# Four chained image layers on one core: first samples' group norms computed a layer earlier, filter stores on GpSimd's queue, a buffer of its own for the single tap's hats, channel sums taken by ScalarE

## The chip, the core and the metric

The kernel runs on one core of one Trainium2 chip. The core has five engines with instruction queues of their own: TensorE (PE; its weight loads are shown apart as PEld), VectorE (DVE), ScalarE (ACT), GpSimd (POOL) and SyncE (SP). PE multiplies matrices into PSUM, the three element-wise engines work on the on-chip memory SBUF, and SP here only issues DMAs, which 16 DMA engines carry out. ACT and POOL can issue DMAs too. Every queue is worked in order: an instruction that waits holds up all behind it.

The metric is the device time of one execution in microseconds. All arithmetic is float32.

## The reference

The input x has 8 samples of 384 channels and 32x32 positions. Four layers follow one another, each of the form x = x + f(group_norm(x)), where the group norm has 32 groups of 12 channels:

```python
x = x + mamba(_gn(x), ...)                 # layer 0
x = x + deform(_gn(x), ...)                # layer 1
x = x + layernorm_mamba_mlp(_gn(x), ...)   # layer 2
x = x + shift_filter(_gn(x), offset)       # layer 3

def _gn(v, G=32, eps=1e-5):
    g = v.reshape(B_, G, C_ // G, H_, W_)
    m = jnp.mean(g, axis=(2, 3, 4), keepdims=True)
    s = jnp.var(g, axis=(2, 3, 4), keepdims=True)
    return ((g - m) / jnp.sqrt(s + eps)).reshape(v.shape)
```

Layers 0 and 2 are state-space layers: a projection to 768 inner channels, a causal convolution of three taps, a scan h = dA * h + dB * u along the 1024 positions for 16 states per channel, a gate and a projection back; layer 2 also has a layer norm in front and an MLP behind. Layer 1 cuts the channels in three blocks of 128 and gives each a deformable depthwise convolution of size K = 3, 5 and 7. Offsets come from an ordinary KxK convolution of the block, every tap then samples the image bilinearly at its shifted place, and a 1x1 convolution follows. A squeeze-and-excitation weight scales the result: it needs each channel's mean and maximum over the positions. Layer 3 shifts groups of channels by given offsets and filters them.

## The kernel before

Channels lie on the 128 partitions in three groups (`G = 3`), positions along the free dimension. Between layers x is kept in DRAM, one tensor per layer.

**Group norm.** `gn_bn` takes DVE's statistics over halves of 512 positions, `gn_aggr` joins them, `gn_mean` (L151) averages mean and variance over a group of channels with a constant matrix `gmat` on PE, `gn_dev` (L171, L173) gives the deviations on DVE, `gn_square` (L178) squares them on ACT, `gn_mean2` (L161) averages the squares on PE, `gn_sum` (L183) and `gn_rstd` (L192 to L195, ACT) give a factor and an offset for each channel. `gn_mean` and `gn_mean2` multiply all nine pairs of 128-channel groups.

**State-space layers** (`ssm_layer`, L211). The work is 16 half-samples ("steps") of 48 units. A unit is a scan of two states on DVE (L546), with its decays on ACT (L526), its inputs on POOL (L534) and the product with C on DVE (L559) or POOL (L557); PE sums the states (L569). `plan` writes by hand, for each step, what each engine does beside unit t: the output projection of the step before, the gate of this one, and the norm, projection and convolution of the next one. Where the next step begins a sample, its x is loaded at t = 0 and its norm runs from t = 2 to t = 9 (`norm_stats`, L303). The last step has no next one. The first step's norm stands alone ahead of the units, at the start of the layer.

**Deformable layer** (`deform_fast`, L1060). Sample 0 is loaded first (L1066). `fir_weights` then loads the 7x7 offset weights (ACT's queue), forms differences of them on POOL (L1201, L1203) and stores the 121 resulting filters in DRAM in nine pieces on ACT's queue (L1209). They serve a fast form of the 7x7 convolution, here called FIR. The loads of the constants of K = 3 and 5 stand on SP's queue, those of K = 7 on ACT's. This part and all of SP's and POOL's instructions are put in order by the framework's scheduler; ACT, PE and DVE keep the order that is written after it.

That order is by slots. A sample has 46 units: 6 for K = 3, 14 for K = 5, 26 for K = 7. `block_steps` puts work into slots with three places before a slot's unit (`act0`, `pe0`, `dve0`) and three after it (`act1`, `dve1`, `pe1`). With t0 the first unit of a sample and s0 that of a block:

- the sample's load at t0-29, statistics to t0-26, means, squares and factors to t0-21 (`stats` L1238, `rstd`), the norm itself (`norm`, L1262) next;
- the 3x3 convolution for offsets at t0-17, the 5x5 one from t0-14 (`conv`, L1382), the FIR in 16 pieces from t0-5, each loaded three slots earlier (`fir_load` L1310, `fir` L1320, `fir_take` L1330 to L1355, `fir_end`);
- around a block change: transposes of the image (L1417, L1424), then, at s0, `sums_act` (L1461) and `sums` (L1466), which empty the accumulators `wacc` of the block before, the 1x1 convolution (L1472, L1478), `squeeze` (L1485 to L1487), and at the end of a sample the scale (L1527) and the store.

A unit samples one quarter (or, for a set with a single tap, one half) of a set of up to eight taps. ACT computes "hats" max(0, 1 - |p - i|) along x and y from the positions (`hats_x` L1665, L1670; `hats_y` L1682, L1687), DVE multiplies them (L1722, into the ring `fsm` of 7 tiles) and weighs the image (L1705), and PE multiplies and adds into `wacc` (L1759). A block begins with its single-tap set, which has two units. Its x hats and those of the other sets share the ring `fhx` of two tiles. For a set whose first unit is u the positions are loaded at u-5 (L1650), x hats come at u-3 and u, y hats at u-2 and u-1.

If an offset is too large for the fast form, `deform_layer` runs instead; it isn't run on this input.

Of the kernel before, what the change touches and what calls it, by code (L numbers as in the profile page):

```python
# [8 lines left out]
F32 = mybir.dt.float32  # L9
AF = mybir.ActivationFunctionType  # L10
ALU = mybir.AluOpType
# [4 lines left out]
P = 128  # L16
# [86 lines left out]
class Net:  # L103
# [12 lines left out]

    def col(self, i):
        return self.cols[:, i : i + 1]
# [28 lines left out]
    def gn_mean(self, mv):  # L147
        ps = self.psum("gn_ps", n=3 * G)
        for g in range(G):
            for k in range(G):  # L150
                self.nc.tensor.matmul(  # L151
                    ps[:, 2 * g : 2 * g + 2], self.gmat[:, k, g * P : (g + 1) * P], mv[:, k, :],
                    start=(k == 0), stop=(k == G - 1),
                )
        return ps

    def gn_mean2(self, dm):
        ps = self.psum("gn_ps2", n=G)
        for g in range(G):
            for k in range(G):  # L160
                self.nc.tensor.matmul(  # L161
                    ps[:, g : g + 1], self.gmat[:, k, g * P : (g + 1) * P], dm[:, k : k + 1],
                    start=(k == 0), stop=(k == G - 1),
# [47 lines left out]
    def ssm_layer(self, li, src, dst, shift=None):  # L211
# [5 lines left out]
        with ExitStack() as ctx:  # L217
# [74 lines left out]
            def norm_load(s):  # L292
                s["xl"] = []
                for h in (1, 0) if s["h"] == 0 else (1,):
                    x = p2.tile([P, G, TS], F32, name="x", tag="x")
                    nc.sync.dma_start(out=x, in_=src(s["b"])[:, :, h * TS : (h + 1) * TS])
# [391 lines left out]
            def plan(prev, s, nxt):  # L688
# [30 lines left out]
                put(pe, 0, norm_load, nxt)  # L719
                if nxt and nxt["h"] == 0:  # L720
                    put(dve, 2, norm_stats, nxt, 0)
                    put(dve, 3, norm_stats, nxt, 1)
                    put(dve, 3, lambda n: n.update(gn_mv=self.gn_aggr(n["gn_st"])), nxt)
                    put(pe, 4, lambda n: n.update(gn_ps=self.gn_mean(n["gn_mv"])), nxt)
                    put(dve, 5, lambda n: n.update(gn_grp=self.gn_dev(n["gn_mv"], n["gn_ps"])), nxt)
                    put(act, 6, lambda n: n.update(gn_dm=self.gn_square(n["gn_grp"][1])), nxt)
                    put(pe, 6, lambda n: n.update(gn_ps=self.gn_mean2(n["gn_dm"])), nxt)
                    put(dve, 8, lambda n: n.update(gn_var=self.gn_sum(n["gn_grp"][0], n["gn_ps"])), nxt)
                    put(act, 9, lambda n: n.update(gn=self.gn_rstd(n["gn_grp"][0], n["gn_var"])), nxt)
# [55 lines left out]
            with tc.manual_schedule(engines=ENGINES):  # L785
# [3 lines left out]
                for i in range(2):  # L789
                    norm_stats(s, i)  # L790
                s["gn"] = s["sib"]["gn"] = self.gn_finish(s["gn_st"])
# [130 lines left out]
    def deform_layer(self, src, dst):  # L922
        tc, nc, ins = self.tc, self.nc, self.ins
        with ExitStack() as ctx:
# [26 lines left out]
            for b in range(self.nb):  # L951
# [28 lines left out]
                for g in range(G):  # L980
                    nc.vector.scalar_tensor_tensor(
                        x[:, g, :], og[:, g, :], se[:, g : g + 1], x[:, g, :], ALU.mult, ALU.add
                    )
                nc.scalar.dma_start(out=dst(b), in_=x)
# [75 lines left out]
    def deform_fast(self, src, dst):  # L1060
        tc, nc, ins = self.tc, self.nc, self.ins
        with ExitStack() as ctx:
# [67 lines left out]
            for u, (b, g, j, h) in enumerate(units):  # L1130
                if h == 0:
                    one = self.parts(g, j) == 2
                    loads[u - 5] = b, g, j
                    for t, fn, k in (
                        ((-3, self.hats_x, 0), (-2, self.hats_y, 0), (-1, self.hats_y, 1))
                        if one
                        else ((-3, self.hats_x, 0), (-2, self.hats_y, 0), (-1, self.hats_y, 1), (0, self.hats_x, 1))
# [966 lines left out]
```

## Time and profile before

| what | value |
|---|---|
| median of 3 runs | 8860.76 us (8858.26 to 8862.39) |
| the profiled execution's own time | 8859.41 us |
| its span, first to last instruction | 8857.3 us |
| mean granted clock of TensorE | 0.906 |
| busy: PE, DVE, ACT, POOL | 84%, 85%, 66%, 63% of the span |

The page of a profile gives busy times by engine and the costliest groups of instructions; the trace behind it answers questions. In a timeline, a row has the start and the duration in microseconds, the engine, the line of the kernel, the operation, what it writes and reads, and how many instructions are merged; brackets hold the idle time of the engine before it, and what ended that time as far as semaphores tell. ACTq and SPq are DMA instructions on the queues of ACT and SP, where the duration of a merged row runs from its first to its last issue. In a row of groups, the busy time and the mean nanoseconds of one instruction follow the count. Durations come from one execution.

### The profile page before, as it was taken

The page shows a single profiled execution, that of the slowest core. Times are in us where ns is not written, and L with a number is a line of the kernel's source. Part 1 is how long each engine was busy: PE and PEld are TensorE (multiplying, and loading weights), DVE is VectorE, ACT ScalarE, POOL GpSimd, SP SyncE. Part 2 cuts the span into 40 slices and gives each one's busy share as a digit, 9 for nine tenths or more (in the row PEclk, how much of TensorE's full clock was granted, in tenths as well). Part 3 has the DMA queues.
Part 4 walks back from the last instruction along what each step waited for, and adds up shares of the span by engine and source line. Part 5 has one row for each costly group of instructions (what it writes and reads, how often), then busy time and mean ns, then how long its engine had stood idle before and what let it go on. Part 6 is the DMA issues. An engine that isn't in the chain of part 4 may idle for free. (4 is left out here: it accounts for less than half of the span.)

```text
span 8857.3 us, 91757 instructions
## 1 busy us (share of the span) xinstructions
PE 7449.8 (84%) x29880; PEld 3853.8 (44%) x29880; DVE 7519.8 (85%) x8477; ACT 5818.6 (66%) x9453; POOL 5565.4 (63%) x3374
## 2 busy tenths in 40 slices
PE   7888888888884899999999975788888888888886
PEld 2232233233221788788788861233333333333332
DVE  6999999999995788988898886888898988888872
ACT  6777777777773656665665655676777777676740
POOL 6999999999996000000000006998898989999954
PEclk8899899899897999999999997898898989999988
DMA  4554555445544554464446434566666566566646
GB/s 127 123 125 120 129 122 124 121 119 124 126 121 112 145 135 125 112 163 131 112 129 159 123 87 104 130 153 150 159 154 149 146 145 154 143 156 157 158 135 112
DMA packets 805681, 1177.71 MB, mean 133 GB/s; under 512 B 267010, under 2 KB 423842, under 8 KB 771400
## 3 DMA queue, kind: packets, MB, share of 16 engines
q1 hardware_dynamic: 742980, 1155.63, 53.0%
q10 hardware_dynamic: 62212, 16.13, 0.9%
q8 instruction: 238, 3.90, 0.2%
q14 instruction: 251, 2.06, 0.1%
HBM read 982.54 MB, written 188.98 MB: 132 GB/s over the span
## 5 line engine op out<-in xcount | busy, mean ns | idle before, releaser
L534 POOL TENSOR_TENSOR db<-dub,bc 128x1024 f32<-128x1024 f32 x1536 | 3608.1, 2358 | 370.7 <-DVE hs L546 170.3
L526 ACT ACTIVATE da<-dtb,vec 128x512 f32<-128x512 f32 x3072 | 2123.4, 691 | 603.1 <-DVE hs L559 403.7
L546 DVE TENSOR_TENSOR_SCAN da<-da,db 128x1024 f32<-128x1024 f32 x960 | 2193.3, 2285 | 130.5 <-ACT da L526 84.0
L467 POOL TENSOR_TENSOR dt<-dt,sp_e 128x512 f32<-128x512 f32 x96 | 122.4, 1275 | 2546.7 <-DVE sp_e L459 2546.7
L1759 PE MATMUL wacc<-fsm,fxk 128*128 128x195 f32 (+21 forms) x10624 | 1575.1, 306 | 151.0 <-ACT fhy L1682 77.2
L1759 PEld LDWEIGHTS wacc<-fsm,fxk 128*128 128x128 f32 x10624 | 1475.9, 195 | 286.9 <-DVE fsm L1722 152.6
L546 DVE TENSOR_TENSOR_SCAN hs<-da,db 128x1024 f32<-128x1024 f32 x576 | 1315.3, 2284 | 195.4 <-POOL db L519 80.8
L557 POOL TENSOR_TENSOR hs<-hs,bc 128x1024 f32<-128x1024 f32 x576 | 1357.8, 2357 | 33.4 <-ACT st L552 33.4
L559 DVE TENSOR_TENSOR hs<-da,bc 128x1024 f32<-128x1024 f32 x960 | 1175.6, 1225 | 126.8 <-PE y L569 77.0
L569 PE MATMUL y<-hs,cols 128*32 128x512 f32 x6144 | 984.0, 650 | 280.3 <-POOL hs L557 258.4
L1722 DVE TENSOR_TENSOR fsm<-fhy,fhx 128x143 f32<-128x143 f32 (+40 forms) x3280 | 1081.9, 397 | 66.8 <-PE wacc L1759 53.0
L1705 DVE TENSOR_TENSOR fxk<-fxt,fwk 128x1024 f32<-128x1024 f32 (+1 forms) x688 | 814.3, 1184 | 10.4 <-PE wacc L1759 5.6
L1682 ACT ACTIVATE fhy<-fpyx,cell 128x416 f32<-128x416 f32 (+10 forms) x832 | 423.8, 582 | 373.7 <-DVE fsm L1722 373.4
L569 PEld LDWEIGHTS y<-hs,cols 128*32 128x32 f32 x6144 | 190.1, 113 | 1006.8 <-issue 491.9
L646 PE MATMUL ps_m<-hid,wm 128*128 128x512 f32 x1152 | 549.3, 632 | 61.9 <-ACT hid L641 27.8
L627 PE MATMUL ps_h<-t,wm 128*128 128x512 f32 x1152 | 530.9, 605 | 44.1 <-DVE sp_e L459 24.6
L1665 ACT ACTIVATE fhx<-fpyx,cell 128x416 f32<-128x416 f32 (+10 forms) x664 | 372.2, 630 | 257.2 <-DVE fsm L1722 252.8
L359 PE MATMUL ps_in<-xn,winr 128*128 128x512 f32 x576 | 327.1, 714 | 174.3 <-ACT xn L348 125.7
L646 PEld LDWEIGHTS ps_m<-hid,wm 128*128 128x128 f32 x1152 | 226.3, 202 | 394.2 <-issue 280.0
L627 PEld LDWEIGHTS ps_h<-t,wm 128*128 128x128 f32 x1152 | 216.1, 193 | 363.0 <-issue 271.5
L578 PE MATMUL ps_z<-xn,winr 128*128 128x512 f32 x576 | 303.0, 674 | 47.8 <-DVE sp_e L459 47.8
L1687 ACT ACTIVATE fhy<-fhy,cols 128x1184 f32<-128x1184 f32 (+8 forms) x208 | 307.6, 1479 | 6.8
(227 smaller groups left out, 9815.7 us busy)
## 6 DMA issues: line engine op xcount, KB each, us to landing
dtb<-dtd SPq DMA_DIRECT2D x768, 256.0 KB
dub<-dtd SPq DMA_DIRECT2D x768, 256.0 KB
fpyx<-fposd SPq DMA_DIRECT2D x104, 1024.0 KB
fxt<-fxd SPq DMA_DIRECT2D x96, 1024.0 KB
wm<-in_w SPq DMA_DIRECT2D x96, 768.0 KB
bc<-bcd SPq DMA_DIRECT2D x256, 256.0 KB
x<-x SPq DMA_DIRECT2D x71, 768.0 KB
dtd<-dt SPq DMA_DIRECT2D x192, 256.0 KB
```

The source lines that it names most:

```text
L526: nc.scalar.activation(da[:, i, :], s["dtb", j][:, k, :], AF.Exp, scale=na[:, j, n + i : n + i + 1])
L534: nc.gpsimd.tensor_tensor(db, du, s["bc"][p][:, 0], ALU.mult)
L546: nc.vector.tensor_tensor_scan(h1, da1, db1, 0.0, ALU.mult, ALU.add)
L557: nc.gpsimd.tensor_tensor(s["hs", m], s["hs", m], c, ALU.mult)
L559: nc.vector.tensor_tensor(hs_tile(s, m), s["da", m], c, ALU.mult)
L569: nc.tensor.matmul(s["y"][k * IP : (k + 1) * IP, :], sel, s["hs", p * NSUB + k][:, i, :], start=mlp and p == 0 and i == 0, stop=p == NQP - ...
L627: nc.tensor.matmul(ps, s["w1", q][:, k, f * P : (f + 1) * P], s["t"][:, k, :], start=(k == 0), stop=(k == G - 1))
L646: nc.tensor.matmul(ps, s["w2", q][:, f, o * P : (o + 1) * P], s["hid", q][:, f, :], start=(f == 0), stop=(f == 3))
L1682: nc.scalar.activation(hy[:, at : at + (yb - ya) * W], s["pyx", j][:, 0, ya * W : yb * W], AF.Abs, bias=bias)
L1705: nc.vector.tensor_tensor(t[:, :n], x, wk[:, j : j + 1, :].to_broadcast([P, n, P]), ALU.mult)
L1722: nc.vector.tensor_tensor(self.sub(sm, at, [(r * w, n), (w, r), (1, w)]), self.sub(hy, hy_at[by] + xa, [(r * W, n), (W, r), (1, w)]), self ...
L1759: nc.tensor.matmul(a[:, ya - 4 * o : yb - 4 * o, xa:xb], k, self.sub(sm, sm_at[by], [(w, yb - ya), (1, w)]), start=o not in s["open"], sto ...
```

## The change

1. Layer 0's last step carries the norm of sample 0 of layer 1, as if it were a next step: two loads of x, the statistics, and so on. The result goes to a new constant tile `gns`. Layer 1 then leaves out this sample's statistics.
2. Sample 0 of layer 1 gets statistics of its output (in `scale`), and its norm for layer 2 is finished 17 to 21 slots after its end, that is in sample 1. Layer 2 then starts with the norm at hand.
3. In `gn_mean` and `gn_mean2` the two pairs of groups that are not neighbours are left out (a group of 12 channels spans at most two of them): 7 products for 9.
4. The nine filter stores go out on GpSimd's queue. For sample 0 the FIR begins two slots later.
5. The single tap's x hats get a buffer `fhs`; the first set after it has its x hats one slot earlier and its positions' load is written one slot earlier; the ring `fsm` has 6 tiles.
6. The channel sums come from the accumulator of ACT's instruction that writes `fog`, in two halves that DVE adds; DVE's sum over 1024 positions is left out.

```diff
+        t = self.const.tile([P, 4, G], F32, name="gns")
+        self.gns = {li: (t[:, li - 1], t[:, li + 1]) for li in (1, 2)}
...
     def gn_mean(self, mv):
-            for k in range(G):
+            ks = [k for k in range(G) if abs(k - g) < 2]
+            for k in ks:
...
# plan, in ssm_layer
-                put(pe, 0, norm_load, nxt)
-                if nxt and nxt["h"] == 0:
-                    put(dve, 2, norm_stats, nxt, 0)
...
+                nn = nxt if nxt or mlp else {"b": 0, "h": 0, "src": dst}
+                put(pe, 0, norm_load, nn)
+                if nn and nn["h"] == 0:
+                    put(dve, 2, norm_stats, nn, 0)
...
+                    to = () if nxt else self.gns[1]
+                    put(act, 9, lambda n: n.update(gn=self.gn_rstd(n["gn_grp"][0], n["gn_var"], *to)), nn)
...
# start of a state-space layer
-                for i in range(2):
-                    norm_stats(s, i)
-                s["gn"] = s["sib"]["gn"] = self.gn_finish(s["gn_st"])
+                if mlp:
+                    s["gn"] = s["sib"]["gn"] = self.gns[2]
+                else:
+                    for i in range(2):
+                        norm_stats(s, i)
+                    s["gn"] = s["sib"]["gn"] = self.gn_finish(s["gn_st"])
...
# deform_fast
-                    loads[u - 5] = b, g, j
+                    lead = 4 if j == 0 else 3
+                    loads[u - 5 if one or j else u - 6] = b, g, j
...
-                        else ((-3, self.hats_x, 0), (-2, self.hats_y, 0), (-1, self.hats_y, 1), (0, self.hats_x, 1))
+                        else ((-lead, self.hats_x, 0), (-2, self.hats_y, 0), (-1, self.hats_y, 1), (0, self.hats_x, 1))
...
# fir_weights
-            nc.scalar.dma_start(out=o, in_=w[:, r0:r1, c0:c1, :].rearrange("p r c o -> p r (c o)"))
+            nc.gpsimd.dma_start(out=o, in_=w[:, r0:r1, c0:c1, :].rearrange("p r c o -> p r (c o)"))
...
# block_steps
-                sample["xn"] = self.xn0
+                sample["xn"], sample["gn"] = self.xn0, self.gns[1]
...
         def point_act():
+            s["sum"] = self.q2.tile([P, 2], F32, name="fos")
-                nc.scalar.activation(og[:, sl], s["pw"][h], AF.Identity, bias=pwb[:, g : g + 1])
+                nc.scalar.activation(
+                    og[:, sl], s["pw"][h], AF.Identity, bias=pwb[:, g : g + 1], accum_out=s["sum"][:, h : h + 1]
+                )
...
-            nc.vector.reduce_sum(am[:, g, 0:1], og, axis=AX.X)
+            nc.vector.tensor_tensor(am[:, g, 0:1], s["sum"][:, 0:1], s["sum"][:, 1:2], ALU.add)
...
         def scale(k):
+            if b == 0:
+                if k == 0:
+                    sample["st"] = self.q1.tile([P, G, 2, 6], F32, name="gn_st0")
+                for h, sl in halves():
+                    nc.vector.bn_stats(sample["st"][:, k, h, :], xr[:, sl])
...
-            put(t0 - 6, "dve1", fir_sum)
-            t = t0 - 5
+            t = t0 - 5 if b else t0 - 3
+            put(t - 1, "dve1", fir_sum)
...
+            if b == 0:
+                sample["to"] = self.gns[2]
+                put(end + 17, "dve1", lambda: sample.update(mv=self.gn_aggr(sample["st"])))
+                for t, place, fn in (
+                    (18, "pe0", mean), (18, "dve1", dev), (19, "act1", square),
+                    (20, "pe0", mean2), (20, "dve1", var), (21, "act1", rstd),
+                ):
+                    put(end + t, place, fn)
...
# hats_x
-        hx = self.q2.tile([P, HXN], F32, name="fhx", tag="fhx")
+        if one:
+            hx = self.q1.tile([P, L], F32, name="fhs", tag="fhs")
+        else:
+            hx = self.q2.tile([P, HXN], F32, name="fhx", tag="fhx")
...
# product, in unit_dve
-            sm = self.q2.tile([P, SMN], F32, name="fsm", tag="fsm", bufs=7)
+            sm = self.q2.tile([P, SMN], F32, name="fsm", tag="fsm", bufs=6)
```

## The prediction

> **What bounds the kernel now.** I read the busy time by stretch first, to part the program into its layers: the first state-space layer to 2790 us, a gap to 2918, the deformable layer to 5280, another gap to 5396, the rest. The rows give length, then busy time (instructions) of PE, PEld, DVE, ACT, POOL, the granted clock, DMA share and GB/s.
>
> ```profile
> 0.00:2790.00 2790.00, 2311.62 (x6972) 810.97 (x6972) 2529.92 (x1693) 2007.06 (x3454) 2544.74 (x1521) 0.89 0.49 120
> 2790.00:2918.00 128.00, 55.86 (x298) 39.05 (x299) 21.05 (x48) 18.70 (x38) 29.10 (x31) 0.69 0.63 170
> 2918.00:5280.00 2362.00, 2207.79 (x14296) 1912.92 (x14294) 2058.37 (x4484) 1470.42 (x2112) 0.00 (x0) 0.97 0.50 129
> ```
>
> DVE and POOL bound the first layer (91% each), PE the second (93%). In the 128 us between them nothing is busy, so the timeline of that gap comes next:
>
> ```profile
> 2806.63 3.66 DVE L1238 BATCH_NORM_STATS2 gn_st<-fxn 128x6 f32<-128x512 f32 x6 [5.31 <-DMA firw<-in_owf]
> ...
> 2812.15 31.01 ACTq L1209 DMA_DIRECT2D fwd<-firw  x9
> ...
> 2855.51 0.17 ACT L178 ACTIVATE gn_dm<-gn_ps 128x3 f32<-128x3 f32 x1 [87.41 <-DMA pwb<-in_pwb]
> ...
> 2860.87 2.26 DVE L1262 TENSOR_SCALAR fxn<-fxn,gn_rstd,gn_nb 128x1024 f32<-128x1024 f32 x3 [0.93 <-ACT gn_nb L195]
> ...
> 2861.78 6.24 PE L1382 MATMUL ps_off<-fxn,fow 128*32 128x256 f32 x72 [2.05 <-issue]
> ```
>
> The sample is in SBUF at 2806.6 and its deviations are ready at 2815.1, but the square that the norm needs waits until 2855.5: on ACT's queue it stands behind nine filter stores (2812 to 2843) and eleven more loads. What follows, on PE alone:
>
> ```profile
> 2869.75 20.11 PE L1382 MATMUL ps_off<-fxn,fow 128*64 128x512 f32 x100 [1.72 <-DVE far L1403]
> 2892.30 4.51 PE L1320 MATMUL ps_off<-fxss,fw 128*98 128x256 f32 x14 [2.44 <-issue]
> ...
> 2918.07 3.40 PE L1759 MATMUL wacc<-fsm,fxk 128*128 128x160 f32 x16
> ```
>
> That is the 5x5 convolution, the first of 16 pieces of the 7x7 filter (FIR), and the first sampled product.
>
> **Norm of layer 1 moved: what the start gains.** Without statistics to wait for, the norm runs at 2806.6, the 3x3 convolution (6.2) ends near 2814, and the 5x5 one starts when its weights have landed: issued at 2815.5, 640 KB at the 235 GB/s of 2810 to 2820 is 3 us, so 2819 to 2839. That is 51 us earlier. But the FIR is next on PE, ahead of the first product, and its loads wait for the filter stores. Today all four first loads leave together at 2847.8, after the ninth store, though their own slices were stored at 2812 to 2815; so I let every load wait for every store. On **GpSimd's queue** the stores stand behind the 18 subtractions, which end at 2831.2 (2829.09 + 2.09). The trace has no DMA issued by GpSimd. Bounds: 6.07 MB (4x784 + 4x588 + 441 KB) at the 304 GB/s of 2835 to 2840 takes 20 us, to 2851. The Trainium skill, DMA: Bandwidth & Descriptors, section "Anatomy of one DMA — SWDGE (gpsimd) path", prices such a DMA at 2.0 us + bytes/436 GB/s: nine in a row would be 18 + 13.9 = 32 us, to 2863. The trace's rate is nearer, since the stores overlap, but two 1 MB position loads now run beside them (2.1 MB, 7 us): I take 2858, and 2861 for the first filter in SBUF. GpSimd itself delays nobody: it has no other work in this layer (0.00 busy). From 2861 three pieces (4.5 cold, then 3.3 each), ACT's take (0.8) and a fourth piece (2.7) put the first product at 2875.6, 42.5 us earlier. Two more pieces than before are left at that point; a slot with a piece costs PE 7.2 us (3.8 + 3.4), and without one DVE sets about 5.5, so 3.4 us come back. **Gain 39 us.** If the filters are ready at 2842 it is 58, if at 2880 it is 20.
>
> Against moving the stores at all speaks the same page, section "Issuing engines are not separate DMA queues": all queues share the 16 engines, and another issuer saves only issue time. By that rule the move is worth nine issues of about 0.4 us, 4 us. The trace says more: ACT issues them over 31 us, as they wait for subtractions and earlier DMAs, and SP's later weights wait 7.6 us for one of them. The rule does hold for the bytes, which is why I let the FIR wait for them.
>
> **What layer 0 pays.** Each odd half-sample there already carries a group norm for the next sample, except the last. Step starts are scans at 2269.51 (with norm) and 2607.76 (the last, without); the thirteenth scans of both:
>
> ```profile
> 2301.78 1.23 DVE L559 TENSOR_TENSOR hs<-da,bc 128x1024 f32<-128x1024 f32 x1 [3.54 <-PE y L569]
> ...
> 2319.43 2.29 DVE L546 TENSOR_TENSOR_SCAN da<-da,db 128x1024 f32<-128x1024 f32 x1
> 2647.65 2.29 DVE L546 TENSOR_TENSOR_SCAN da<-da,db 128x1024 f32<-128x1024 f32 x1
> ```
>
> 49.9 us against 39.9: a norm costs 10 us. Six statistics (3.7) and small operations (0.9) lie on DVE, which has no slack, and PE waits for the means, so that read-outs come late and DVE stalls 3.5 and 2.2 us. The two 768 KB loads on SP are in that difference too, with the 4.5 us that POOL then waits for `dub`.
>
> ```profile
> 2285.41 4.00 PE L151 MATMUL gn_ps<-gn_mv,gmat 128*128 128x2 f32 x18 [8.23 <-DVE gn_mv L143]
> ```
>
> Of its 18 instructions 14 are left, 0.9 us less on that chain: the last step pays 10.0 - 0.9 = **+9.1**, seven others gain 0.9, **-6.2**, and the start of layer 0 gains both times, **-1.8**. In layer 2 PE waits there for `wm` (5.4 us at 7993), which hides the first saving; the second is worth some 0.2 us a sample, **-1**. In layer 1 it falls where DVE is behind: 0.
>
> **Single-tap buffer and earlier hats.** PE's largest stall in the deformable layer is 9.7 us before each 7x7 block, eight times (seven are 67.6 us in the waits from 3050 to 5280):
>
> ```profile
> 3634.45 2.43 ACT L1665 ACTIVATE fhx<-fpyx,cell 128x352 f32<-128x352 f32 x4
> 3636.90 1.84 ACT L1670 ACTIVATE fhx<-fhx,cols 128x1856 f32<-128x1856 f32 x1
> 3638.65 1.11 ACT L1461 COPY fdsb<-wacc 128x448 f32<-128x448 f32 x3
> 3639.80 1.93 DVE L1466 TENSOR_TENSOR fdsb<-fdsb,wacc 128x320 f32<-128x320 f32 x4 [4.03 <-ACT fdsb L1461]
> 3641.87 7.96 PE L1759 MATMUL wacc<-fsm,fxk 128*128 128x288 f32 x16 [9.66 <-ACT fhy L1682]
> ```
>
> The waits' label is not the cause: the accumulators must be emptied (ACT, then DVE), and ACT comes to it late, after the next set's x hats (4.3 us) and the second y hats (3.4). The change puts those x hats one slot earlier, ahead of the y hats. The total before the copy is the same; only ACT's wait for DVE at 3631.1 (1.47 us) is filled. The positions' load is no obstacle, it leaves at 3615.9. **8 x 1.5 = -12**. At the other two block changes the FIR keeps PE busy: 0. The products' ring falls from 7 to 6. DVE waited for it 42 times (50.0 us), nearly always where PE is ahead in work; where the program makes DVE wait for PE, four tiles are ready in either case. Bounds: 0, or one tile of PE work (2.1 us) per wait, 42 x 2.1 = 88. I take **+4**.
>
> **Sums by ACT.**
>
> ```profile
> L1485 DVE TENSOR_REDUCE am<-fog 128x1 f32<-128x1024 f32 x22 | 26.7, 1213 | 0.0
> ```
>
> A sum of 1.21 us becomes an addition of about 0.16. Of three per sample only that of the 5x5 block lies where DVE is behind (busy without a break 3642 to 3742, PE waiting 1.4 us at 3690): 8 x 1.05 = **-8.4**; at the end of the layer all three engines wait for the last one: **-1**. The accumulation on ACT has no row; between 0 and one further 0.69 us pass per half, hidden behind ACT's slack (62% busy), 1.4 us exposed only at the end: I take 0.
>
> **Norm of layer 2 moved.**
>
> ```profile
> 5302.71 0.92 SPq L228 DMA_DIRECT2D x<-x  x2
> ...
> 5307.71 3.66 DVE L303 BATCH_NORM_STATS2 gn_st<-x 128x6 f32<-128x512 f32 x6 [5.01 <-issue]
> ...
> 5323.06 2.21 ACT L310 ACTIVATE xn<-x,gn_nb,gn_rstd 128x512 f32<-128x512 f32 x3
> ```
>
> The second half of x is there by 5309.5 at the latest; with the norm's factors ready ACT can apply them from about 5308.8, **-14.3**, and all behind it is a chain. The weights, issued from 5305.2, are needed only near 5327. The price is in sample 1 of layer 1: six statistics (4.1 us) where DVE waits for PE anyway, 0.9 us of DVE and a few ACT operations with table loads (1.28 each) near a 7x7 start: between 0 and 6, **+2**.
>
> **Sum.** -39 + 9.1 - 6.2 - 1.8 - 1 - 12 + 4 - 8.4 - 1 - 14.3 + 2 = -68.6. The profiled execution took 8859.41 us, 2.1 more than its span of 8857.3, and lies 1.35 below the median of 8860.76. So 8860.8 - 68.6, about **8792 us**.
>
> **Rivals.** *Filters are no bound* (the first stores get in between the subtractions): the start gains 58, 8773 us; for it, the first slices need few subtractions, against it, today's loads waited for the last. *GpSimd stores slowly*, or SP stands before the filter loads with positions queued behind: gain 20, 8811 us; for it, SP issues in order and waited 6.4 us for `fwd` at 2847.8. *The smaller ring couples DVE to PE*, slower: the place is the product-to-matmul hand-over of 368 units; it decides when a unit loses 0.20 us ((68.6 + 4) / 368), about 35 of those 42 waits becoming a tile's stall each. At the full 88 us instead of 4, 8876 us; against it, PE waits for DVE only 63.6 us in 2230.
>
> **How the numbers follow.** The likeliest has a chance of 0.52, filters early 0.15, stores slow 0.22, the ring 0.06; 0.05 is left for no measurable change. Each of the first three is faster even with 30 us off. Some 0.2% (18 us) is what a measurement here tells from no change. The range reaches from filters early with the other sixteen sums worth their full 1.05 us too (8773 - 17 = 8756) to slow stores with a third of the ring's cost (8811 + 25 = 8836).
>
> **What would show it.** Right: the 3x3 convolution starts near 2809 (everything comes 1 us later after layer 0), the first FIR piece near 2862, the first product near 2877; the last step of layer 0 has 49 us to its thirteenth scan; PE's stall before 7x7 blocks is 8.2; xn follows x by a microsecond in layer 2. Wrong: a first FIR piece after 2880, DVE waits on the ring that turn into PE waits for `fsm`, or a convolution still held by its weights or x.

## The result and the profile after

The changed kernel takes 8791.62 us (median of 4 runs, 8789.68 to 8796.0), the kernel before 8859.51 us (4 runs, 8855.55 to 8862.39): a ratio of 0.9924, 95% interval 0.9907 to 0.9942, or 68 us. The forecast was 8792. The sum is right to half a microsecond, but not because each of its terms was. The profiled execution took 8793.49 us, its span is 8791.7, 65.6 less than before.

The windows of the profile after, cut where its stretches end (layer 0's last scan, the first sampled product, the last one); columns as in the prediction:

```profile
0.00:2779.00 2779.00, 2259.12 (x6890) 793.72 (x6890) 2530.81 (x1701) 2009.24 (x3460) 2544.12 (x1519) 0.89 0.51 121
2779.00:2881.00 102.00, 61.49 (x281) 33.87 (x280) 27.62 (x35) 14.95 (x26) 36.91 (x40) 0.80 0.66 189
2881.00:5236.00 2355.00, 2211.77 (x14296) 1913.61 (x14294) 2047.29 (x4501) 1476.88 (x2172) 0.00 (x0) 0.97 0.51 131
```

The gap between layers 0 and 1 is shorter by a third, layer 0 is longer, the deformable layer hardly shorter. The same cuts through both traces, with the prediction's terms put where they belong (the saving of sample 0 counted in the second row). A first product is counted from its weight load here and below, 0.2 us ahead of its own row:

| stretch | before, us | after, us | difference | predicted |
|---|---|---|---|---|
| start to layer 0's last scan | 2769.1 | 2778.7 | +9.6 | +1.1 |
| to the first product of sample 1 | 444.4 | 403.5 | -40.9 | -41.1 |
| sample 1 | 300.0 | 303.0 | +3.0 | 0 |
| samples 2 to 7 | 1766.6 | 1750.7 | -15.9 | -12.3 |
| last product to layer 2's first load | 22.6 | 20.6 | -2.0 | -1.0 |
| that load to layer 2's first scan | 92.8 | 79.7 | -13.1 | -14.3 |
| layers 2 and 3 from there | 3461.8 | 3455.5 | -6.3 | -1.0 |
| sum | | | -65.6 | -68.6 |

The start of layer 1 after, from the timeline:

```profile
2815.18 4.44 DVE L1275 TENSOR_SCALAR fxn<-fxn,gns 128x1024 f32<-128x1024 f32 x3 [5.36 <-DMA fobk<-in_c_cols]
...
2816.89 5.38 PE L1395 MATMUL ps_off<-fxn,fow 128*32 128x256 f32 x72 [18.24 <-DMA fobk<-in_c_cols]
...
2833.11 21.91 PE L1395 MATMUL ps_off<-fxn,fow 128*64 128x512 f32 x100 [10.84 <-DMA fow<-in_ow]
...
2840.32 5.26 POOL L1222 DMA_DIRECT2D fwd<-firw  x7
...
2859.63 0.43 DVE L1297 TENSOR_TENSOR fxss<-fxq 128x256 f32<-128x256 f32 x1
...
2864.08 5.47 PE L1333 MATMUL ps_off<-fxss,fw 128*98 128x256 f32 x18 [3.56 <-DMA fw<-fwd]
...
2881.25 3.40 PE L1792 MATMUL wacc<-fsm,fxk 128*128 128x160 f32 x16
```

The norm follows the sample at once (2815.2 instead of 2860.9). Then there are two waits in place of the one: the 5x5 convolution for its weights (10.8 us), and the first FIR piece for the filters. Seven of the nine stores are issued only at 2840.3 to 2845.6, after GpSimd's last subtraction, and have landed by 2860.6: some 5.0 MB in 20.3 us, 247 GB/s. SyncE issues the first filter load at 2860.62.

In the deformable layer, at a 7x7 start, and then at layer 2's start:

```profile
3601.25 2.43 ACT L1698 ACTIVATE fhx<-fpyx,cell 128x352 f32<-128x352 f32 x4
...
3608.77 1.11 ACT L1474 COPY fdsb<-wacc 128x448 f32<-128x448 f32 x3
...
3611.98 4.48 PE L1792 MATMUL wacc<-fsm,fxk 128*128 128x288 f32 x9 [8.07 <-ACT fhy L1715]
...
5256.47 0.92 SPq L233 DMA_DIRECT2D x<-x  x2
...
5263.48 2.22 ACT L315 ACTIVATE xn<-x,gns 128x512 f32<-128x512 f32 x3 [16.53 <-DMA wx<-in_wx]
```

The x hats now stand 7.5 us ahead of the copy that empties the accumulators, and PE's stall is 8.07 us (before 9.66). In layer 2, xn follows the load of x by 7.0 us (before 20.4).

### The profile page after: what moved, and what is told of

The parts are those of the page before. It is cut to its first block, busy times and chain, and to the rows that moved or that the text cites. A ratio compares the mean times of both kernels' runs of the same rounds, so it can differ in the third digit from the quotient of the medians.

```text
span 8791.7 us, 91535 instructions
## 1 busy us (share of the span) xinstructions
PE 7389.6 (84%) x29688; PEld 3814.4 (43%) x29688; DVE 7510.6 (85%) x8477; ACT 5818.7 (66%) x9501; POOL 5571.8 (63%) x3383
## 5 line engine op out<-in xcount | busy, mean ns | idle before, releaser
L551 DVE TENSOR_TENSOR_SCAN da<-da,db 128x1024 f32<-128x1024 f32 x960 | 2193.3, 2285 | 129.9 <-ACT da L531 86.9
L1755 DVE TENSOR_TENSOR fsm<-fhy,fhx 128x585 f32<-128x585 f32 (+39 forms) x3136 | 1007.6, 383 | 92.9 <-PE wacc L1792 89.9
L1698 ACT ACTIVATE fhx<-fpyx,cell 128x352 f32<-128x352 f32 (+9 forms) x640 | 344.3, 609 | 237.0 <-DVE fsm L1755 222.8
L583 PE MATMUL ps_z<-xn,winr 128*128 128x512 f32 x576 | 303.0, 674 | 47.7 <-DVE sp_e L464 47.7
```

The costliest lines, as they stand in the source:

```text
L551: nc.vector.tensor_tensor_scan(h1, da1, db1, 0.0, ALU.mult, ALU.add)
L1755: nc.vector.tensor_tensor(self.sub(sm, at, [(r * w, n), (w, r), (1, w)]), self.sub(hy, hy_at[by] + xa, [(r * W, n), (W, r), (1, w)]), self ...
```

## Experiments

Each run starts from the changed kernel, but for two that start from the one before. Times are medians of five runs or more. Where a few microseconds count, stretches of the traces are compared, since one and the same kernel gave 8791.62 us on one occasion and 8794.08 on another.

**Stores back on ScalarE's queue.**

```diff
-            nc.gpsimd.dma_start(out=o, in_=w[:, r0:r1, c0:c1, :].rearrange("p r c o -> p r (c o)"))
+            nc.scalar.dma_start(out=o, in_=w[:, r0:r1, c0:c1, :].rearrange("p r c o -> p r (c o)"))
```

> The changed kernel, but the nine filter stores go out on ScalarE's queue again. If GpSimd's queue is what brings the filters in time (the reading behind the prediction), the first product comes at least 5 us later after layer 0's last scan than the 102.6 us of the changed kernel, and the time is 8797 or more. Rival: once the norm no longer waits on ScalarE, the queue of the stores is indifferent or better there, since each store may leave as soon as its subtractions are done and need not wait for all 18: the last store has landed by about 2850 instead of 2860.6, the first FIR piece is then bound by the 5x5 convolution (DVE's last input to it ends at 2860.1) and starts 0 to 4 us earlier than 2864.1; time 8788 to 8793.

8800.34 us, 0.994 times before (0.9926 to 0.9953). The first product comes 113.1 us after layer 0's last scan (changed kernel: 102.3 and 106.0 in two traces). The timeline says why:

```profile
2819.11 32.94 ACTq L1222 DMA_DIRECT2D fwd<-firw  x9
...
2863.24 6.38 PE L1333 MATMUL ps_off<-fxss,fw 128*98 128x256 f32 x18 [2.66 <-DMA fw<-fwd]
...
2867.46 0.47 ACTq L1124 DMA_DIRECT2D cell<-in_c_cell  x1
2868.03 1.07 ACT L1437 COPY fxt<-ps_t 128x512 f32<-128x512 f32 x2 [92.67 <-DMA pwt<-in_pw]
```

The filters are no later (first piece 86.9 us after layer 0's end, against 85.4 and 87.2), so the first reading is wrong in its reason. But eleven further loads stand behind the stores on ScalarE's queue, and its first copy and hats behind those: ready at 2868 instead of 2859.8. With the norm already moved, GpSimd's queue is worth some 7 us, by freeing ScalarE, not by bringing the filters sooner.

**Layer 1's norm back in layer 1.**

```diff
-                nn = nxt if nxt or mlp else {"b": 0, "h": 0, "src": dst}
+                nn = nxt
...
-                sample["xn"], sample["gn"] = self.xn0, self.gns[1]
+                sample["xn"] = self.xn0
...
-            if b > 0:
+            if True:
```

> The changed kernel, but layer 1 takes the statistics of its first sample itself, as before, and layer 0's last step has no norm in it. Layer 0 gets its 9.5 us back on each theory. If moving the norm is what gained the start, the first product comes 25 to 45 us later after layer 0's last scan than 102.6 us, and the time is 8807 to 8825. Rival: the wait before was made by the stores on ScalarE's queue, and with these on GpSimd's the norm is ready some 10 to 20 us after the sample, behind ScalarE's loads; the 5x5 convolution had to wait for its weights until 2833 anyway, so the first product comes 8 to 15 us later after layer 0's end, and the time is 8790 to 8797.

8787.36 us (8786.15 to 8789.81), 0.9926 times before (0.9913 to 0.994), so the kernel is no slower without this part of the change.

```profile
2821.47 0.17 ACT L183 ACTIVATE gn_dm<-gn_ps 128x3 f32<-128x3 f32 x1 [56.52 <-DMA f<-in_fc]
...
2829.06 6.28 PE L1395 MATMUL ps_off<-fxn,fow 128*32 128x256 f32 x72 [4.21 <-POOL firw L1216]
...
2862.43 4.76 PE L1333 MATMUL ps_off<-fxss,fw 128*98 128x256 f32 x18
```

Layer 0 ends at 2766.0 (the other runs with seven products and no norm in the last step: 2766.3 and 2765.9; the seven with it: 2776.0 to 2778.7, mean 2777.1). So the moved norm costs layer 0 11.0 us. It gains 4.9: to sample 1's first product it is 408.4 us without, 403.5 and 403.3 with it. As a part of its own it loses some 6 us. The square now waits for ScalarE's loads, until 10.7 us after its deviations, and the first FIR piece comes 96.4 us after layer 0's end (85.4 and 87.2).

**The kernel before with the stores on GpSimd's queue alone.**

```diff
-            nc.scalar.dma_start(out=o, in_=w[:, r0:r1, c0:c1, :].rearrange("p r c o -> p r (c o)"))
+            nc.gpsimd.dma_start(out=o, in_=w[:, r0:r1, c0:c1, :].rearrange("p r c o -> p r (c o)"))
```

> The kernel before with one edit: the nine filter stores go out on GpSimd's queue. From layer 0's last scan to sample 1's first product the kernel before took 444.4 us, the changed one 403.5, with its norm back in layer 1 408.4, with its stores back on ScalarE's queue 410.2. If stores and norm each take away the same wait, this edit alone gives nearly all of the gain at the start: the norm's square follows ScalarE's loads instead of the stores, the stretch becomes 410 to 416 (the filter keeps its earlier slots here, some 3 us), the time 8857.7 - 32 = 8823 to 8830. Rival: the two add up, and the stores alone gain only 6 to 7 us of it, which is what they were worth with the norm moved: 8851.

8829.46 us, 0.9966 times before (0.9954 to 0.9978). The stretch is 415.0 us, 29.4 less than before. So this one edit brings 29 of the 41 us. With the other parts in place as well, stores without the norm bring 36 (408.4), the norm without the stores 34 (410.2), both 41. The two take away the same wait.

**Layer 2's norm back in layer 2, and nothing of it in sample 1.**

```diff
-                if mlp:
-                    s["gn"] = s["sib"]["gn"] = self.gns[2]
-                else:
-                    for i in range(2):
-                        norm_stats(s, i)
-                    s["gn"] = s["sib"]["gn"] = self.gn_finish(s["gn_st"])
+                for i in range(2):
+                    norm_stats(s, i)
+                s["gn"] = s["sib"]["gn"] = self.gn_finish(s["gn_st"])
...
-                for h, sl in halves():
-                    nc.vector.bn_stats(sample["st"][:, k, h, :], xr[:, sl])
```

> The changed kernel, but layer 2 takes its first sample's statistics itself, as before, and sample 0 of layer 1 has none of its output. The stretch from layer 2's first load to its first scan goes from 79.7 back to about 93 us (+13). If the extra operations in sample 1 are what makes that sample's period 303.0 us against 297.3 of the later ones, it goes to 297.3 to 298, and the time is 8791.6 + 13 - 5.5 = 8799. Rival: sample 1 is long for another reason (the filter of sample 0 comes two slots later and leaves work over); its period stays at 302 to 303, and the time is 8805.

8798.92 us, 0.9939 times before (0.9926 to 0.9953). From layer 2's first load to its first scan 90.6 us (changed: 79.7), sample 1 takes 297.3 (303.0). The second is as expected; the first gives back 10.9 us, where 13 were expected. Sample 1's price in the changed kernel, on PE and DVE:

```profile
3274.13 1.29 DVE L1548 BATCH_NORM_STATS2 gn_st<-fxr 128x6 f32<-128x512 f32 x2
...
3277.14 9.48 PE L1792 MATMUL wacc<-fsm,fxk 128*128 128x154 f32 x64 [3.13 <-DVE fsm L1755]
...
3296.27 3.12 PE L155 MATMUL gn_ps<-gn_mv,gmat 128*128 128x2 f32 x14 [4.13 <-DVE gn_mv L146]
```

PE waits for DVE behind the statistics, and for the averages' input just ahead of the 7x7 block. With the averages' own time the sample is 5.7 us longer for it.

**DVE sums again.**

```diff
-            nc.vector.tensor_tensor(am[:, g, 0:1], s["sum"][:, 0:1], s["sum"][:, 1:2], ALU.add)
+            nc.vector.reduce_sum(am[:, g, 0:1], og, axis=AX.X)
```

> The changed kernel, but DVE sums the 1024 positions again, and ScalarE's accumulator isn't read. The prediction's term is 1.05 us for each sample (the 5x5 block's sum alone) and 1 at the end: the period of samples 2 to 7 goes from 297.3 back to 298.4, and the time to about 8801. Rival 1: all three sums of a sample were on the path, period 300, time 8815. Rival 2: none was, and the whole saving of 2.7 us per sample comes from the single tap's buffer and the earlier hats: period 297.3, time 8793.

8801.81 us, 0.9942 times before (0.9929 to 0.9956). Samples 2 to 6 take 298.3 to 298.4 us, the last 265.2 (264.2), the tail 22.2 (20.6). So the saving is that of one sum a sample, as the prediction had it; that it is the 5x5 block's is not shown. Both new instructions, by line, in the changed kernel:

```profile
L1501 DVE TENSOR_TENSOR am<-fos x24: 143/150/159, 2933.8 to 5243.6; 128x1 f32<-128x1 f32 x24
```

```profile
L1492 ACT ACTIVATION_READ_ACCUMULATOR fog<-ps_pw,pwb x48: 188/193/195, 2927.6 to 5243.4; 128x1 f32 x48
```

(Durations are minimum, median and maximum in ns.)

**Single tap back in the shared ring, hats at their old place.**

```diff
-        if one:
-            hx = self.q1.tile([P, L], F32, name="fhs", tag="fhs")
-        else:
-            hx = self.q2.tile([P, HXN], F32, name="fhx", tag="fhx")
+        hx = self.q2.tile([P, HXN], F32, name="fhx", tag="fhx")
...
-                    lead = 4 if j == 0 else 3
-                    loads[u - 5 if one or j else u - 6] = b, g, j
+                    lead = 3
+                    loads[u - 5] = b, g, j
```

> The changed kernel, but the single tap's x hats share the ring of two tiles again, and the set after it has its x hats and its positions' load where they were before. The prediction's term is 1.5 us at each of eight 7x7 starts: PE's stall there goes from 8.2 back to 9.7, the period of samples 2 to 7 from 297.3 to 298.8, and the time to about 8803. What the run with DVE's sums left for it says much the same: 2.7 - 1.05 = 1.65 us a sample, 298.9. Rival: the hats save nothing, since the accumulators are emptied as late as before, and the rest of the 2.7 us comes from the norm's seven products in each sample: period 297.3, time 8792.

8807.31 us, 0.9942 times before (0.9928 to 0.9956). Samples 2 to 6 take 298.9 (three) or 300.0 us (two), in the mean 2.0 more than with the tap's own buffer; the stall is back:

```profile
3608.27 2.42 ACT L1695 ACTIVATE fhx<-fpyx,cell 128x352 f32<-128x352 f32 x4
...
3612.47 1.11 ACT L1474 COPY fdsb<-wacc 128x448 f32<-128x448 f32 x3
...
3615.70 6.52 PE L1789 MATMUL wacc<-fsm,fxk 128*128 128x288 f32 x15 [9.65 <-ACT fhy L1712]
```

**Six tiles in the ring of the kernel before.**

```diff
-            sm = self.q2.tile([P, SMN], F32, name="fsm", tag="fsm", bufs=7)
+            sm = self.q2.tile([P, SMN], F32, name="fsm", tag="fsm", bufs=6)
```

> The kernel before with one edit: the products' ring has 6 tiles. The prediction's term is +4 us in all (0.5 us a sample), the period 300.0 goes to 300.5. Rival (the slower one of the prediction): a tile's stall at each of 42 waits, 11 us a sample, period 311, time 88 us above the kernel before. Third: PE never runs out of finished products for it, DVE only waits more often, and the period stays at 300.0. In layers 2 and 3, which this edit doesn't touch, the trace also tells whether the 6.3 us that the changed kernel had there are its doing (3148.2 + 313.6 us from the first scan on as in the trace of before) or scatter (nearer to 3143.7 + 311.8).

8859.84 us, 1.0003 times before (0.9995 to 1.0012). DVE's waits for the ring and PE's for products, in seven samples (us in total, number, longest): first with seven tiles, then with six.

```profile
DVE fsm L1722 <- PE wacc L1759: 50.0, 42, 1.7
PE wacc L1759 <- DVE fsm L1722: 63.6, 91, 2.4
```

```profile
DVE fsm L1722 <- PE wacc L1759: 79.2, 105, 1.9
PE wacc L1759 <- DVE fsm L1722: 65.7, 101, 2.4
```

DVE's waits grow from 42 to 105 and from 50.0 to 79.2 us, PE's by 2.1 us only. Samples 1 to 6 take 300.4 to 300.8 us, and the stretch from first to last product 2366.5 against 2362.2: +4.3.

**All nine pairs of groups.**

```diff
-            ks = [k for k in range(G) if abs(k - g) < 2]
+            ks = list(range(G))
```

> The changed kernel, but both averages of the group norm multiply all nine pairs of channel groups again. The prediction's terms are 0.9 us in each of layer 0's steps with a norm (eight with the moved one: 7.1), 1.8 at layer 0's start, 1 in layer 2, nothing in layer 1: the last scan of layer 0, 2776 to 2779 in the seven runs with the moved norm so far, comes at 2785 to 2788, and the time is 8794 + 10 = 8804. Rival: in layer 0 PE's averages are done before the DMA that GpSimd waits for in the same steps, so that only the start pays: last scan at 2778 to 2782; what the runs with nine and with seven products differ by in layers 2 and 3 (3458 to 3462 us against 3453 to 3456) is then the larger part, and the time is 8798 to 8802. Third: that difference is scatter, 8795 to 8797.

8804.2 us, 0.9937 times before (0.9923 to 0.9951): the size was right, the places were not. Layer 0 ends at 2781.2, 4.1 later than the mean of the seven. Samples 1 to 7 take 2059.8 us against 2053.7, layers 2 and 3 3458.4, 2.6 more than the mean of ten traces with seven products (3455.8). So 4, 6 and 3 us, where the prediction had 9 of 10 in layer 0 and none in layer 1. Layer 0's end lies where the rival had it, but not for the rival's reason (see below). And the 6 us of layer 1 are not clearly the products': samples 2 and 3 take 297.3 us as with seven, the rest are samples 4 to 6, longer by 1.1 to 2.1 us, and sample 1. Single samples longer by 1.1 us occur in runs without any change to these products too (two in the run with the stores alone, one in that with layer 1's own norm); their cause is open.

**Sample 0's filter with the others' slots.**

```diff
-            t = t0 - 5 if b else t0 - 3
+            t = t0 - 5
```

> The changed kernel, but the 7x7 filter of sample 0 has its 16 pieces from five slots ahead, as for the other samples. By the prediction's working two more pieces (some 6.6 us) then stand ahead of the first product, and two slots less have a piece afterwards (3.4 us each way in its sum): the first product comes 5 to 7 us later, sample 0's period of 301.2 us is 3.4 to 7 shorter, and the time is 8792 to 8796. Rival: the pieces are hidden behind DVE in the slots of sample 0, so that they cost nothing there: the first product later by 6, the period the same, time 8798.

8797.94 us, 0.9934 times before (0.992 to 0.9947). First product 114.3 us after layer 0's end, sample 0 296.4 us. The two traces of the changed kernel have 102.3 and 301.2, and 106.0 and 297.3: so 12 us are lost and 4.8 come back by the first, 8.3 and 0.9 by the second. By both, sample 1 starts 7.3 us later (410.7 against 403.5 and 403.3). Of this, 2 to 4 us are a first piece that came later here (89.3 against 85.4 and 87.2), which the edit need not have caused. The shift is worth 3 to 7 us; the prediction's two terms leave 3.2. The time is the rival's.

**A version to beat both.** Layer 1's norm in layer 1, ScalarE's late loads on GpSimd's queue, layer 2's norm in other units of sample 1.

```diff
-            nc.scalar.dma_start(out=self.cell, in_=ins["c_cell"])
+            nc.gpsimd.dma_start(out=self.cell, in_=ins["c_cell"])
...
-                put(end + 17, "dve1", lambda: sample.update(mv=self.gn_aggr(sample["st"])))
+                put(end + 28, "dve1", lambda: sample.update(mv=self.gn_aggr(sample["st"])))
```

> A version meant to beat both: layer 1's norm taken in layer 1 (layer 0's last step without it), ScalarE's loads of the 7x7 block's taps, of the 1x1 and squeeze weights and of the cell constants moved to GpSimd's queue behind the filter stores, so that the square of the norm follows its deviations; and the norm for layer 2 made in units 28 to 38 of sample 1 instead of 17 to 21. If those loads are what held the square (2810.8 to 2821.5 in the run with layer 1's own norm), the first product comes 8 to 11 us earlier after layer 0's end than 112.4; the filters, last stored 81.8 us after it, allow a first FIR piece at 85 instead of 96.4. If the place of the norm for layer 2, at the start of the 7x7 block, is what costs, sample 1's period goes from 303.3 to 298 to 299. Both: 8787.4 - 9.5 - 5 = 8773. Rival: the 5x5 convolution's weights, or the cell constants now behind nine stores, take the place of the wait, and the operations cost the same wherever DVE sets the pace: 8785 to 8788.

8800.72 us, 0.9935 times before (0.9921 to 0.9949): 13 us worse than without these edits, as is the stretch to sample 1's first product (422.0 against 408.4).

```profile
2814.33 13.06 POOL L1217 TENSOR_TENSOR firw<-firw 128x1078 f32<-128x1078 f32 x6
...
2818.94 10.53 DVE L1276 TENSOR_SCALAR fxn<-fxn,gns 128x1024 f32<-128x1024 f32 x3 [0.93 <-ACT gns L200]
...
2827.34 5.41 POOL L1223 DMA_DIRECT2D fwd<-firw  x7
...
2849.66 0.58 POOL L1125 DMA_DIRECT2D cell<-in_c_cell  x1 [0.93 <-DMA fwd<-firw]
2850.24 0.17 POOL L1127 MEMSET far<- 128x64 f32 x1
...
2851.70 21.47 PE L1396 MATMUL ps_off<-fxn,fow 128*64 128x512 f32 x100 [16.74 <-DVE far L1418]
```

```profile
L1276 DVE TENSOR_SCALAR fxn<-fxn,gns x3: 817/875/8996, 2818.9 to 2828.6; 128x1024 f32<-128x1024 f32 x3
```

(The second view has minimum, median and maximum in ns.) The square came at once, as meant, but two new waits took its place. DVE's first product of the norm took 9.00 us, the next two 0.82 and 0.88; it ended 0.6 us after GpSimd's subtractions (2827.3). And each of the eight loads on GpSimd's queue but the first waited for a store to land, so that a small memset behind them held DVE, and with it PE, until 2850. Sample 1 went from 303.3 to 302.0 only, so the place of the later operations was worth 1.3 us; the statistics stayed where they were.

**The same with SyncE for the loads and ScalarE for sample 0's norm.**

```diff
-            nc.gpsimd.dma_start(out=self.cell, in_=ins["c_cell"])
+            nc.sync.dma_start(out=self.cell, in_=ins["c_cell"])
...
+            if b == 0:
+                nc.scalar.activation(x, x, AF.Identity, bias=m[:, i : i + 1], scale=r[:, i : i + 1])
+                return
             nc.vector.tensor_scalar(x, x, r[:, i : i + 1], m[:, i : i + 1], ALU.mult, ALU.add)
```

> Layer 1's norm taken in layer 1 as in the run that gained by it, and the norm for layer 2 in units 28 to 38; ScalarE's loads of the taps, weights and cell constants now on SyncE's queue, and the three products that apply the norm to sample 0 done by ScalarE. In the run with those loads on GpSimd's queue the norm's factors were ready at 2818.9, but DVE's first product took 9.0 us for 0.8, until GpSimd's subtractions had ended, and the 5x5 convolution then waited until 2851.7 for a small GpSimd operation that stood behind the loads. If it is DVE's place beside GpSimd that costs (two engines that hold each other up in SBUF), ScalarE's three products take about 1 us each and the 3x3 convolution starts near 2820, 54 us after layer 0's end instead of 63; the filters, last stored near 2848, then bind the first FIR piece (2851 to 2855, 85 to 89 after the end, against 96.4), and the time is 8776 to 8780. Rival: the wait belongs to data (a load, a semaphore) and not to the engine: ScalarE waits as long, or SyncE's longer queue makes the 5x5 convolution's weights late; 8785 or more.

8787.2 us (8783.58 to 8787.94), 0.9918 times before (0.9904 to 0.9932).

```profile
2817.08 3.49 ACT L1276 ACTIVATE fxn<-fxn,gns 128x1024 f32<-128x1024 f32 x3
2818.41 6.45 PE L1398 MATMUL ps_off<-fxn,fow 128*32 128x256 f32 x72 [2.70 <-issue]
...
2859.53 1.15 ACT L1701 ACTIVATE fhs<-fpyx,cell 128x1024 f32<-128x1024 f32 x1 [4.84 <-DMA fpyx<-fposd]
```

Beside the same subtractions ScalarE is not held up, and the first FIR piece comes at 87.9 us after layer 0's end instead of 96.4. Then the positions are late, on SyncE's longer queue, and the first product gains only 3.4 us (109.0). So the DVE half of the expectation held, and the time is the rival's (8785 or more): no better than the 8787.36 us of the run that only takes layer 1's norm back.

> The changed kernel itself, on the chip of the two runs before it, so that the version above is compared with it directly. 0.9924 times the kernel before, and the same stretches: 102 to 107 us from layer 0's last scan to the first product, a period of 297.3 us from sample 2 on, 301 and 303 for samples 0 and 1.

8794.08 us (8791.15 to 8795.93) on the same chip, 0.9927 times before (0.9914 to 0.9941). The stretches are as expected but for sample 0: 297.3 us, not 301. The first trace's 301.2 goes with its earlier first product (102.3 us, here 106.0), and both reach sample 1 together (403.5 and 403.3). The version above is 6.9 us faster, with ranges that don't overlap; that is 0.08%, below what was called a measurable change.

## Why the prediction came out right

**The start of layer 1 (-39): right in size, half right in its reason.** Counted from layer 0's last scan, the prediction had the first product at 106.3 us; the two traces have 102.3 and 106.0. The filters bound the first FIR piece, as it said, so the rival in which they don't is out, and so is the one with slow stores: they landed 81.9 us after layer 0's end, where the prediction had 88.9. What failed is hidden by that: "the 5x5 one starts when its weights have landed", 2819, was 2833. The cause is in SyncE's instructions: a small load waited 7.4 us for the load of x, until 2815.0, and the weights behind it left at 2822.8 instead of 2815.5:

```profile
SPq L1102 <- DMA fxn<-x: 7.4, 1, 7.4
```

```profile
2814.97 0.27 SPq L1102 DMA_DIRECT2D fgrid<-in_c_grid  x1
...
2822.82 0.59 SPq L1097 DMA_DIRECT2D fow<-in_ow  x1
```

The filters cover most of it, since DVE has the FIR's input by 2860.1 and PE can start on it only at 2864.1.

The larger gap is that the prediction priced norm and stores as one gain. Each without the other takes away most of the same wait (36 and 34 of 41 us), so only one of them was needed, and the one that costs layer 0 11 us was not it. The rule of the Trainium skill that was weighed there (DMA: Bandwidth & Descriptors, section "Issuing engines are not separate DMA queues"), by which another issuer saves only issue time (4 us by the prediction's estimate), is near what the stores' move is worth beside the moved norm (6.7 us of this stretch), and far from what it is worth alone (29.4), because on ScalarE the norm's own work stood behind them.

**What layer 0 pays (+9.1 - 6.2 - 1.8): the second term failed.** The last step with a norm takes 170.9 us (161.4 before): +9.5. The 0.9 us that the prediction took off for fewer products are not in it, since the run with all nine takes 170.8. Nor did the other seven gain 0.9 us each: together they take 1215.6 us before and 1216.7 after. PE's and DVE's rows of one such step after, then PE's row of the output projection before:

```profile
2285.53 3.15 PE L155 MATMUL gn_ps<-gn_mv,gmat 128*128 128x2 f32 x14 [11.02 <-DVE gn_mv L146]
...
2288.53 10.71 PE L606 MATMUL ps_o<-u,wout 128*128 128x512 f32 x18
...
2300.03 1.92 PE L574 MATMUL y<-hs,cols 128*32 128x512 f32 x16
...
2301.97 1.23 DVE L564 TENSOR_TENSOR hs<-da,bc 128x1024 f32<-128x1024 f32 x1 [3.62 <-PE y L574]
```

```profile
2289.27 9.78 PE L601 MATMUL ps_o<-u,wout 128*128 128x512 f32 x18
```

The averages are shorter by 0.85 us, as worked out, but the 18 products that follow them at once take 0.93 us more. So `y`, which stands behind them on PE, is no earlier, and DVE's stall behind it is 3.62 us (3.54 before). The windows, before and after, show PE's clock behind the averages (third figure from the end of a row):

```profile
2291.40:2293.40 2.00, 2.00 (x4) 0.73 (x4) 1.97 (x4) 1.62 (x5) 0.00 (x0) 0.62 0.90 180
2293.40:2295.40 2.00, 2.00 (x6) 0.86 (x5) 1.97 (x3) 0.81 (x5) 0.57 (x1) 1.00 0.06 13
```

```profile
2291.50:2293.50 2.00, 2.00 (x3) 0.74 (x3) 1.97 (x4) 1.60 (x5) 0.00 (x0) 0.50 1.02 208
2293.50:2295.50 2.00, 2.00 (x5) 0.90 (x4) 1.97 (x3) 0.82 (x5) 0.24 (x1) 0.86 0.15 28
```

The averages run at a granted clock of 0.50 in both kernels, after PE has stood idle for 8 to 11 us. With fewer of them PE reaches the projection sooner, but still at half clock, and does more of it there. In the later steps of twelve traces `y` starts 14.4 to 14.6 us after the averages began, with nine products and with seven. The load of `dub`, which GpSimd waits for in this step, does not set it: GpSimd's product ends at 2299.5 before and 2299.9 after, and `y` starts when PE's own row ahead of it is done. The failing step of the prediction is thus "0.9 us less on that chain", multiplied by seven: a shorter row on PE was taken for an earlier end of PE's chain.

Over several traces the seven steps save 2.3 us instead of 6.2 (means of four with nine products and ten with seven), and the start of layer 0 saves 1.3 instead of 1.8. In all of layer 0 the seven products save 4.4 us (mean end 2770.5 in three traces with nine, 2766.1 in three with seven).

**Hats (-12), ring (+4), sums (-8.4 and -1): right, the hats somewhat more.** Undone, they cost 2.0, 0.5 and 1.06 us a sample in the mean of samples 2 to 6 (predicted 1.5, 0.5 and 1.05). Hats and sums less the ring are 2.6 of the measured 2.7, which leaves nothing to speak of for the seven products; their term for layer 1, 0, may be right. The slower rival, by way of the ring, fails although the number of DVE's waits more than doubled: PE's own waits for products grew by 2.1 us in seven samples.

**Layer 2's norm (-14.3, +2).** The start gained 13.1: x took 7.0 us to be used, not 6.1. Some of this is scatter, since four traces with this norm in layer 2 have 90.6 to 92.8 us there. The term for sample 1 was mis-sized, 5.7 instead of 2, since "where DVE waits for PE anyway" doesn't hold where the statistics stand. The part still gains.

**Layers 2 and 3 (-1).** Traces of kernels with nine products scatter from 3457.9 to 3461.8 us, with seven from 3453.4 to 3459.9; the means differ by 4.0. Of the 6.3 us some 2 are scatter; why the rest is 4 and not 1 is not shown.

So the prediction missed 8.5 us in layer 0, 3.0 in sample 1 and 1.2 at layer 2's start on one side, and 3.6 in samples 2 to 7, 5.3 in layers 2 and 3 and 1.0 in the tail on the other. The time was met to half a microsecond because they nearly cancel, and that is luck.

## What to carry to other kernels

Where a change takes away one wait in two ways, price each with the other in place: here the cheap one did nearly all, and the costly one was a loss beside it. A row that gets shorter is worth something only if what stands behind it on the same engine does not get longer: where PE has just been idle, read the granted clock of the rows behind before multiplying a saving by the number of steps. A load or a small memset put behind stores on a queue waits with them, and so does whoever needs it.

## What was not expected of the hardware

Layer 0's steps hold a length of their own. In each of six traces looked at, all changes of PE's granted clock lie on one grid of 3.413 us. Two half-samples together, from one norm to the next, settle at 337.9 us, which is 99 of these, with nine products and with seven, whether the first pairs are longer (339.0, 338.4, 338.2, 338.0, 337.9 in the run with the stores alone) or shorter (336.6, 337.3, 337.6, 337.7, 337.9 in the second trace of the changed kernel). This fits steps that are tied to the clock's grid, so that a saving made at half clock is lost again. No run took the clock's changes away, so the tie is argued and not shown.

Some DVE operations took far longer beside GpSimd's subtractions, with no wait in the program between the two. In the first version above a product of 128x1024 took 9.00 us instead of 0.82, over four subtractions of 2.08 to 2.44 us that followed one another; in the changed kernel an addition of a single column took 3.98 us, and the norm's products 1.5 each. The Trainium skill, "SBUF — State Buffer", section "Who interferes with whom", says that the two engines share a pair of SBUF ports, that a `tensor_scalar` or an operation with two SBUF inputs on DVE can need it, that the first to issue keeps it for its whole instruction, and that ScalarE never waits on anyone. The rows agree: ScalarE's three products took 3.49 us, and six BATCH_NORM_STATS2 of DVE, with one input, 3.66 us beside them. But DVE was held for four instructions of GpSimd, not for one. That the port is the cause is argued from these rows; no run took it away alone. The prediction's "GpSimd itself delays nobody" was wrong by it.

ScalarE's accumulator output is a second instruction of 0.19 us, small beside the bound of 0.69 us that the prediction allowed.
